# A four-layer graph network on one core: matrix for 4500 destinations instead of 5000, and four jobs moved to other queues and stages

## The chip, the cores and the metric

The kernel runs on one core of one Trainium2 chip. The metric is the time of one execution on the device, in microseconds (us). The kernel before takes 3546.83 us, the median of three runs (3539.9 to 3551.82). One more execution was taken with the hardware profiler, and all durations below come from it. PE is the matrix engine (PEld its weight loads), DVE the vector engine, ACT the scalar engine, POOL GpSimd, and SP the sync engine, which here only issues DMAs.

## The reference, cut to what matters

There are N = 6250 nodes with 128 features and E = 106250 directed edges, sorted by destination (`dst`); each node has one edge to itself at least. Four layers follow each other, each with a residual and a layernorm:

```python
edge_index = jnp.stack([src, dst])
x = _layernorm(x + _L0_gnn_ref(x, edge_attr_128, src, dst, ...))   # MLP of [sum over edges of edge_attr_128, x]
x = _layernorm(x + _L1_gnn_ref(x, edge_index, ...))                # h = (1+eps) x + sum of x[src]; MLP with two batchnorms
x = _layernorm(x + _L2_gnn_ref(x, edge_index, ...))                # two means of x[src], each with two matmuls
x = _layernorm(x + _L3_gnn_ref(x, edge_index, edge_attr_16, ...))  # attention over the edges of a node, 3 heads
```

Three sums over the edges of a node have the same form, `jax.ops.segment_sum(x[src], dst)`: one in layer 1 and two in layer 2 (called layers 2a and 2b below). Layer 3 forms a logit for each edge from three terms, `a_src[row2] + a_dst[col2] + a_edge`, with `a_edge` from `edge_attr_16` (for a node's own edge from the mean over its edges), and takes a softmax over the edges of each node.

## The kernel before, in words

**Layer 0's stage and the matrix.** 70 batches of `edge_attr_128` are loaded by SP's queue and summed by destination with one-hot matmuls (`by_group`). Into the same loop is woven `making` (L620): it builds, for the first `ND` = 5000 destinations, the 0/1 adjacency matrix from nodes to destinations, in bf16. It does so in steps: DVE makes two one-hots (`olow` and `okey`, L616), PE multiplies them (`made`, four matmuls, L643), ACT copies the product into a stage (L645) and stores that to DRAM through its own queue. There are 13 steps for 250 destinations, 260 in all. The matrix lies in DRAM as 10 parts of 500 destinations.

**An aggregation.** `neighbours` (L778) runs three times. For each of the matrix' parts it loads ten pieces of 625 KB by SP's queue, and for each piece PE makes 15 matmuls (L845; 150 for a part, features split in three bf16 pieces as the stationary operand `xp`, written by `split`). The destinations that the matrix doesn't hold (1250 of them, 61 groups) are handled by `gathered()`: `fetch` has POOL's queue gather their source rows from a table in DRAM with indirect DMAs, 128 rows each (L800; three for a group, 183 in all), eight groups' buffers deep; then for each quad of four groups PE sums with one-hots (`both`, L341), ACT copies to `by_node` (L343), PE transposes (L345) and DVE adds (L348). `due` spreads the quads over the pieces; `others()` waits for all that remain and then handles their parts. In layers 1 and 2a `others()` comes after the last part of the matrix, in layer 2b before its last two. After a part's sum, `take`/`then` do what the layer needs with its 500 destinations.

**What else shares these stages.** `logits` loads `edge_attr_16` in 28 slices (`eat`, L691 and L693) on POOL's queue during layer 1's aggregation, with the products on DVE (L683, L684). `counting` (L524) and `counted` (L549) find where each node's edges begin: an iota on POOL (L542), compares on DVE (L544, L546), small matmuls (L536), all in layer 1's aggregation; then 50 gathers of `nd` on POOL (L436) and 13 compares and reductions on DVE (L563, L564), in layer 1's MLP and layernorm. `loops` sums `a_edge` along the edges and stores `esum`; `last_sums` (L663) gathers from it 50 times (`st`, L665, POOL) in layer 2a's aggregation. In layer 2b, `then` forms for each part the rows for layer 3 and scatters `a_dst` to the first edge of each node, four indirect DMAs on POOL (`edst`, L1071); its buffers `xw` and `ad` are partly filled by POOL memsets first (L1048, L1049). Layer 3 loads `edst` (L1102), spreads it along the edges by a scan, fetches rows for all 831 tiles of edges (L1090) and works through 208 windows.

**The order.** Every engine executes its own list of instructions in a fixed order that the framework's scheduler sets when the program is built; a queue's DMAs are issued in the order of the engine that issues them. Waits are on semaphores.

Of the kernel before, what the change touches and what calls it, by code (L numbers as in the profile page):

```python
# [8 lines left out]
F32 = mybir.dt.float32  # L9
# [34 lines left out]
SC = 250  # L44
ND, Q0 = 5000, 54
AN = N - ND + SC + GW
# [163 lines left out]
def by_windows(ctx: ExitStack, tc: tile.TileContext, a: dict, out: bass.AP, consts, ix):  # L210
# [22 lines left out]
    x3 = dram.tile([NW, XW], F32, name="x3")  # L233
    edst = dram.tile([RB * L, 4], F32, name="edst")
    esum = dram.tile([RB * L, H], F32, name="esum")
# [172 lines left out]
    nc.gpsimd.memset(acc0, 0.0)  # L408
    nc.scalar.dma_start(edst.rearrange("(p t) f -> p (t f)", t=L), acc0[:RB, 0:L * 4])
    loan = [NB5 * F // 2]  # L410
# [137 lines left out]

    def counted(pool):  # L549
# [22 lines left out]
        p = (yield).tile([128, 4, F], F32, name="node_p")[:, 0, :]  # L572
        start = p[:PB, 0:NB5]
# [100 lines left out]
    def logits(pool, work):  # L674
# [11 lines left out]
        for c in range(0, L, W):  # L686
            x = work.tile([RB, W, 16], F32, name="eat")
            n = min(W, max(0, E - full - c))
            if n < W:
                nc.gpsimd.memset(x, 0.0)  # L690
            nc.gpsimd.dma_start(x[0:RB - 1], ea[0:full, :].rearrange("(p t) k -> p t k", t=L)[:, c:c + W, :])  # L691
            if n:
                nc.gpsimd.dma_start(x[RB - 1:RB, 0:n, :],  # L693
                                    ea[full + c:full + c + n, :].rearrange("(p t) k -> p t k", p=1))
# [10 lines left out]
    make = making(mkp, mps)  # L705
    product = products()
    quads, batches, LATE = ND // SC * 13, (NG + 3) // 4, 6
    for q in range(batches):
# [21 lines left out]
        if q in (8, 12):  # L730
            next(product)
    for _ in make:
        pass
    keep.close()

    with tc.tile_pool(name="l0w", bufs=2) as work, \
# [131 lines left out]
    with tc.tile_pool(name="l1", bufs=1) as wp:  # L868
# [37 lines left out]
        with tc.tile_pool(name="l1d", bufs=1) as dp, tc.tile_pool(name="l1e", bufs=4) as two, \  # L906
# [17 lines left out]
            for x in (logit, indices):  # L924
                for _ in x:
                    pass
        counts = ExitStack()
        degrees = counted(counts.enter_context(tc.tile_pool(name="l1c", bufs=1)))
        next(degrees)
        with tc.tile_pool(name="l1p", bufs=1) as lp, tc.tile_pool(name="l1w", bufs=2) as work, \  # L930
# [4 lines left out]
            for k in range(len(PARTS)):  # L935
# [11 lines left out]
                if k in (2, 4):  # L947
                    next(looped)
        batchnorm(2, s2, b2, g2, be2)
        with tc.tile_pool(name="l1x", bufs=2) as work, tc.tile_pool(name="zps", bufs=3, space=bass.MemoryType.PSUM) as zps, \  # L950
                tc.tile_pool(name="tps", bufs=2, space=bass.MemoryType.PSUM) as tp:
            last = None
            for blocks in CHUNKS:
# [7 lines left out]
                if last is not None:  # L961
                    last()
                degrees.send(work)
                layernorm(xn[:PB, b0:b0 + nb, :], z)
# [5 lines left out]
            last()  # L970
            degrees.send(zps)
        counts.close()

    with tc.tile_pool(name="l2", bufs=1) as wp, tc.tile_pool(name="l2w", bufs=2) as work, \
# [49 lines left out]

        ends = last_sums()
        neighbours(before, take, None, tables[1], len(matrix), lambda i: next(ends, None))
        for _ in ends:
            pass  # L1030


    with tc.tile_pool(name="l2bw", bufs=2) as work, \
# [8 lines left out]
        def then(k):  # L1042
            blocks = CHUNKS[k]
            b0, nb = blocks[0], len(blocks)
            x = xn[:PB, b0:b0 + nb, :]
            xw = work.tile([128, 4, XW], F32, name="xw")
            ad = work.tile([128, 4, 4], F32, name="ad")
            nc.gpsimd.memset(xw[:, :, F + H:XW], 1.0)  # L1048
            nc.gpsimd.memset(ad, 0.0)  # L1049
            s = nodes(xt[:, cols(k)], nb, tp)  # L1050
# [19 lines left out]
            for j in range(nb):  # L1070
                nc.gpsimd.indirect_dma_start(  # L1071
                    out=edst, out_offset=bass.IndirectOffsetOnAxis(ap=start_of[:PB, b0 + j:b0 + j + 1], axis=0),
                    in_=ad[:PB, j, :], in_offset=None)
# [845 lines left out]
```

## Time and profile before

| what | value |
|---|---|
| median of three runs | 3546.83 us (3539.9 to 3551.82) |
| profiled execution, its own time | 3244.44 us |
| its span in the trace | 3242.7 us |
| mean granted clock of PE | 0.892 |
| busy: PE / DVE / POOL / ACT | 2522.9 / 1720.1 / 1670.9 / 899.5 us |

The profiled execution is 302 us shorter than the median of the runs without a profiler; nothing in the trace says where these lie. By time from the span's start the stages are: layer 0's sums and the matrix, 30 to 473 us; layer 0's MLP, to 632; layer 1's aggregation, to 1021; its MLP and layernorm, to 1158; layer 2a, to 1640; layer 2b, to 2090; layer 3, to 3243. A row of the groups reads: line, engine, operation, output and inputs with shapes, count | busy time, mean duration in ns | idle time of the engine just before, with what ended it.

### The profile page before, as it was taken

How to read it: one execution, taken by the hardware profiler on the slowest of the kernel's cores; microseconds unless marked ns; L12 is line 12 of the kernel's file. 1: busy time of each engine (PE TensorE's matmuls, PEld its weight loads, DVE VectorE, ACT ScalarE, POOL GpSimd, SP SyncE). 2: the span in 40 equal slices, each digit the busy share in tenths (PEclk: the TensorE clock that was granted, in tenths of full speed). 3: DMA queues.
4: the chain of work that ended last, by engine and by line, in shares of the span. 5: the costliest groups of instructions: out<-in, count | busy, mean ns of one | idle time of the engine just before them, and what ended most of it. 6: DMA issues, size and time to landing. Idle time of an engine off the chain costs nothing.

```text
span 3242.7 us, 42918 instructions
## 1 busy us (share of the span) xinstructions
PE 2522.9 (78%) x14960; PEld 1531.4 (47%) x14960; DVE 1720.1 (53%) x4633; ACT 899.5 (28%) x1661; POOL 1670.9 (52%) x1690
## 2 busy tenths in 40 slices
PE   3888989878999576999988899566666677666665
PEld 2444446534444233454543344255555566555555
DVE  4878865469313830000031112277778688877776
ACT  0788874300001410000120001023323233333332
POOL 5000001167633467653056762467777777777773
PEclk9889889989999677999999899778888898888888
DMA  6699871377763264666366665422323333233321
GB/s 190 204 306 304 295 255 39 105 211 234 224 207 100 68 173 116 209 198 191 106 202 179 178 198 172 107 54 68 71 63 73 69 71 71 69 69 70 70 68 39
DMA packets 334829, 461.82 MB, mean 142 GB/s; under 512 B 45310, under 2 KB 219166, under 8 KB 334245
## 3 DMA queue, kind: packets, MB, share of 16 engines
q1 hardware_dynamic: 251420, 278.88, 29.7%
q0 software_dynamic: 54912, 105.86, 13.4%
q10 hardware_dynamic: 28270, 74.24, 6.2%
q8 instruction: 120, 1.97, 0.3%
q14 instruction: 107, 0.88, 0.1%
HBM read 375.30 MB, written 83.36 MB: 141 GB/s over the span
## 4 chain that ended last, share of the span: by engine, by line
PE 30%; DVE 14%; issue 7%; DMA 7%; POOL 6%; ACT 3%; DVEq 1%; ACTq 0%; POOLq 0%; SPq 0%
PE sums L845 16%; PE o L1198 6%; DMA rows<-x,srca 4%; DVE w L1186 3%; POOL rows L1090 3%; DVE w L1171 3%; POOL row L800 2%; ACT w L1188 2%; PE yp L1020 1%; PE w_p L1176 1%; DVE mx L1179 1%; PE fp L1132 1%; DMA row<-table,srca 1%; PE both L341 1%; POOL st L665 1%
## 5 line engine op out<-in xcount | busy, mean ns | idle before, releaser
L845 PE MATMUL sums<-piece,arena 125*128 125x500 bf16 x4500 | 998.2, 379 | 10.4 <-DMA piece<-edges 10.4
L1090 POOL DMA_INDIRECT rows<-x,srca x831 | 843.1, 1015 | 274.3 <-issue 173.4
L845 PEld LDWEIGHTS <-arena 125*128 125x128 bf16 x4500 | 433.4, 98 | 530.0 <-issue 49.8
L800 POOL DMA_INDIRECT row<-table,srca x549 | 537.9, 980 | 262.8 <-issue 129.4
L1198 PE MATMUL o<-rows,w 128*120 128x132 f32 x2078 | 358.1, 312 | 247.7 <-ACT w L1188 247.5
L1198 PEld LDWEIGHTS o<-rows,w 128*120 128x120 f32 x2078 | 308.1, 211 | 290.7 <-ACT w L1188 290.2
L645 ACT CAST arena<-made 128x1000 bf16<-128x1000 f32 (+1 forms) x260 | 315.6, 1277 | 58.8 <-PE made L643 57.0
L1188 ACT ACTIVATE w<-w 128x720 f32<-128x720 f32 x208 | 167.0, 803 | 435.1 <-DVE w L1186 398.2
L643 PE MATMUL made<-okey,olow 128*128 128x250 bf16 x1000 | 257.7, 400 | 35.5 <-ACT arena L645 16.5
L343 ACT COPY by_node<-both 128x128 f32<-128x128 f32 (+1 forms) x48 | 12.7, 265 | 764.0 <-PE both L341 726.9
L1176 PE MATMUL w_p<-ident,w 128*120 128x128 f32 x1248 | 200.5, 297 | 25.4 <-DVE w L1171 23.3
L1179 DVE TENSOR_REDUCE mx<-w_p 120x1 f32<-120x768 f32 x208 | 197.3, 949 | 18.3 <-PE w_p L1176 17.4
L1171 DVE TENSOR_TENSOR w<-oh,z 128x720 f32<-128x720 f32 x208 | 186.8, 898 | 8.3 <-PE o L1198 6.2
L352 DVE TENSOR_TENSOR onehot<-iota,relg 128x384 f32<-128x384 f32 x118 | 63.8, 543 | 235.8 <-PE both L341 221.7
L1186 DVE TENSOR_TENSOR w<-w,both 128x720 f32<-128x720 f32 x208 | 186.4, 896 | 3.0 <-PE both L1183 2.6
L1176 PEld LDWEIGHTS w_p<-ident,w 128*120 128x120 f32 x1248 | 159.6, 150 | 57.0 <-DVE w L1171 25.5
L716 POOL MEMSET ea<- 128x128 f32 x1 | 0.2, 208 | 357.3 <-PE sums L341 357.3
L643 PEld LDWEIGHTS <-olow 128*128 128x128 bf16 x1000 | 109.9, 119 | 157.2 <-issue 69.2
L616 DVE TENSOR_TENSOR okey<-iok,key 128x1000 bf16<-128x1000 bf16 (+1 forms) x260 | 169.4, 652 | 0.0
L1156 DVE TENSOR_TENSOR z<-rows,zed 128x12 f32<-128x12 f32 x208 | 34.1, 164 | 196.0 <-DMA rows<-x,srca 195.8
L341 PE MATMUL both<-row,onehot 128*32 128x128 f32 x1098 | 55.0, 299 | 104.1 <-DVE arena L348 60.1
L1148 PE MATMUL o<-zeros 128*120 128x380 bf16 x416 | 126.1, 351 | 10.2 <-POOL zeros L1112 8.6
(286 smaller groups left out, 3305.6 us busy)
## 6 DMA issues: line engine op xcount, KB each, us to landing
piece<-edges SPq DMA_DIRECT2D x300, 625.0 KB
edges<-arena ACTq DMA_DIRECT2D x100, 625.0 KB
ea<-in_edge_attr_dram SPq DMA_DIRECT2D x69, 768.0 KB
loop<-x SPq DMA_DIRECT2D x208, 68.0 KB
rows<-x,srca POOLq DMA_INDIRECT x831
row<-table,srca POOLq DMA_INDIRECT x549
eat<-in_edge_attr_dram POOLq DMA_DIRECT2D x28, 236.0 KB
table<-xn SPq DMA_DIRECT2D x24, 224.0 KB
```

Source lines behind the costliest of these rows:

```text
L616: nc.vector.tensor_tensor(o[:, :, 0:n], numbers[:, :, 0:n], of.rearrange("p (o g) -> p o g", o=1).to_broadcast([128, m, n]), op=OP.is_equal)
L643: nc.tensor.matmul(p[:, i, 0:NB5 * GD], lhsT=o[:, :, i], rhs=w[:, :, i], start=True, stop=True)
L645: nc.scalar.copy(to, p[:, 0:n, 0:NB5 * GD].rearrange("p i (h d) -> p i h d", d=GD))
L800: nc.gpsimd.indirect_dma_start(out=r[:, j, :], out_offset=None, in_=table, in_offset=bass.IndirectOffsetOnAxis(ap=ix["src"][:, t:t + 1], a ...
L845: nc.tensor.matmul(p, lhsT=xp[:PB, h, i, :], rhs=t[:PB, :, (h - h0) * SC:(h - h0 + 1) * SC], start=(h == 0 and i == 0), stop=(h == NB5 - 1 ...
L1090: nc.gpsimd.indirect_dma_start(out=r[:, j, :], out_offset=None, in_=x3, in_offset=bass.IndirectOffsetOnAxis(ap=ix["src"][:, BT * b + j:BT ...
L1171: nc.vector.tensor_tensor(w, oh.to_broadcast([128, S, H, BW]), z.rearrange("p j (h w) -> p j h w", w=1).to_broadcast([128, S, H, BW]), op= ...
L1176: nc.tensor.transpose(tp[:, j // 3, j % 3 * 128:(j % 3 + 1) * 128], w[:, j, :, :].rearrange("p h w -> p (h w)"), ident)
L1179: nc.vector.tensor_reduce(mx, tp[:, :, 0:384], AX.XY, OP.max)
L1186: nc.vector.tensor_tensor(wf, wf, mb.rearrange("p (j h) w -> p j (h w)", j=1) .to_broadcast([128, S, H * BW]), op=OP.subtract)
L1188: nc.scalar.activation(wf, wf, AF.Exp)
L1198: nc.tensor.matmul(o[:, 0:F + H + 1], lhsT=wf[:, j, :], rhs=rr, start=(j == 0), stop=(j == S - 1))
```

## The change

There are six edits.

1. `ND` goes from 5000 to 4500 (and `Q0` with it): nine parts of the matrix instead of ten, and 81 groups of fetched destinations instead of 61.
2. `counting` runs in layer 0's stage beside the matrix build (one of its eleven calls at batches 15, 20, ... 65), with buffers of its own; `counted` runs in layer 0's MLP.
3. The loads of `eat` are issued by ACT's queue, their memset by DVE.
4. `last_sums` issues its 50 gathers in one go at the end of layer 1's MLP.
5. `xw` and `ad` are three fixed buffers, filled once by DVE.
6. The scatters of `a_dst` alternate between two tensors; layer 3 loads both and adds them.

```diff
-ND, Q0 = 5000, 54
+ND, Q0 = 4500, 49
...
-    edst = dram.tile([RB * L, 4], F32, name="edst")
+    edst = [dram.tile([RB * L, 4], F32, name=f"edst{i}") for i in range(2)]
...
-    nc.scalar.dma_start(edst.rearrange("(p t) f -> p (t f)", t=L), acc0[:RB, 0:L * 4])
+    for x in edst:
+        nc.scalar.dma_start(x.rearrange("(p t) f -> p (t f)", t=L), acc0[:RB, 0:L * 4])
...
     def counting(pool, psum):
-        row = tail[:RB, AN:AN + M * PB]
-        view = arena[:RB, NB5 * 3 * F + 2 * (AN + M * PB):]
+        row = pool.tile([RB, M * PB], F32, name="node_row")
+        view = pool.tile([RB, 2 * M * PB], BF16, name="node_below")
...
-                p = psum.tile([128, 2 * SC], F32, name="hp1")
+                p = psum.tile([128, 256], F32, name="counts")
...
     def last_sums():
         for b in range(NB5):
             nc.gpsimd.indirect_dma_start(
                 out=st[:PB, b, :], out_offset=None, in_=esum,
                 in_offset=bass.IndirectOffsetOnAxis(ap=lasti[:PB, b:b + 1], axis=0))
-            yield
...
     def logits(pool, work):
...
-                nc.gpsimd.memset(x, 0.0)
-            nc.gpsimd.dma_start(x[0:RB - 1], ea[0:full, :]...)
+                nc.vector.memset(x, 0.0)
+            nc.scalar.dma_start(x[0:RB - 1], ea[0:full, :]...)
...
-    product = products()
+    product, indices = products(), counting(gw, pp1)
...
     for q in range(batches):
...
-    for _ in make:
-        pass
+        if q >= 13 and q % 5 == 0:
+            next(indices, None)
+    for x in (make, indices):
+        for _ in x:
+            pass
...
         nc.gpsimd.memset(xp[96:128], 0.0)
+        degrees = counted(cp)
+        next(degrees)
         for blocks in CHUNKS:            # layer 0's MLP
...
+            degrees.send(work)
         last()
+        degrees.send(yps)
...
-            logit, indices = logits(dp, two), counting(dp, hps)
+            logit = logits(dp, two)
             def each(i):                 # layer 1's aggregation
-                if i % 7 == 1:
-                    next(indices, None)
                 if i % 3 == 2:
                     next(logit, None)
...
-        degrees = counted(counts.enter_context(tc.tile_pool(name="l1c", bufs=1)))
-        next(degrees)
...
+            last_sums()                  # end of layer 1's MLP
         batchnorm(2, s2, b2, g2, be2)
...
-        ends = last_sums()
-        neighbours(before, take, None, tables[1], len(matrix), lambda i: next(ends, None))
-        for _ in ends:
-            pass
+        neighbours(before, take, None, tables[1], len(matrix))
...
+        ads = xws.tile([128, 3, 4, 4], F32, name="ad")
+        xws = xws.tile([128, 3, 4, XW], F32, name="xw")
+        nc.vector.memset(xws[:, :, :, F + H:XW], 1.0)
+        nc.vector.memset(ads, 0.0)
...
         def then(k):                     # layer 2b
-            xw = work.tile([128, 4, XW], F32, name="xw")
-            ad = work.tile([128, 4, 4], F32, name="ad")
-            nc.gpsimd.memset(xw[:, :, F + H:XW], 1.0)
-            nc.gpsimd.memset(ad, 0.0)
+            xw, ad = xws[:, k % 3], ads[:, k % 3]
...
-                    out=edst, out_offset=bass.IndirectOffsetOnAxis(ap=start_of[:PB, b0 + j:b0 + j + 1], axis=0),
+                    out=edst[j % 2], out_offset=bass.IndirectOffsetOnAxis(ap=start_of[:PB, b0 + j:b0 + j + 1], axis=0),
...
-        ed = fp.tile([RB, L, 4], F32, name="ed")
-        for p0, p1, queue in ((0, 112, nc.sync), (112, RB, nc.scalar)):
-            queue.dma_start(ed[p0:p1].rearrange("p t f -> p (t f)"),
-                            edst[p0 * L:p1 * L, :].rearrange("(p t) f -> p (t f)", t=L))
+        ed, more = (fp.tile([RB, L, 4], F32, name=n) for n in ("ed", "edm"))
+        for to, x, queue in ((ed, edst[0], nc.sync), (more, edst[1], nc.scalar)):
+            for p0, p1 in ((0, 112), (112, RB)):
+                queue.dma_start(to[p0:p1].rearrange("p t f -> p (t f)"),
+                                x[p0 * L:p1 * L, :].rearrange("(p t) f -> p (t f)", t=L))
+        nc.vector.tensor_add(ed, ed, more)
```

In the program as built, two orders follow. `st`'s gathers stand on POOL between the row fetches of layer 1 and those of layer 2a (before: in front of the second pair of quads of layer 2a). And with `nd` gone from layer 1's stage, SP issues the first five pieces of layer 2a earlier, and about 150 of layer 2a's `sums` matmuls, one part, stand in PE's list among the transposes of layer 1's layernorm (before: none).

More of the change, by code (lines that the diff above doesn't have):

```diff
@@ L571, in counted @@
             nc.vector.tensor_scalar(shift[:, i, :], iota[:PB, :PB], nxt[:PB, i:i + 1], None, op0=OP.is_equal)
-        p = (yield).tile([128, 4, F], F32, name="node_p")[:, 0, :]
+        p = (yield).tile([128, 4, F], F32, name="yp")[:, 0, :]
         start = p[:PB, 0:NB5]
@@ L689, in logits @@
             if n < W:
-                nc.gpsimd.memset(x, 0.0)
-            nc.gpsimd.dma_start(x[0:RB - 1], ea[0:full, :].rearrange("(p t) k -> p t k", t=L)[:, c:c + W, :])
+                nc.vector.memset(x, 0.0)
+            nc.scalar.dma_start(x[0:RB - 1], ea[0:full, :].rearrange("(p t) k -> p t k", t=L)[:, c:c + W, :])
             if n:
-                nc.gpsimd.dma_start(x[RB - 1:RB, 0:n, :],
+                nc.scalar.dma_start(x[RB - 1:RB, 0:n, :],
                                     ea[full + c:full + c + n, :].rearrange("(p t) k -> p t k", p=1))
@@ L731, in by_windows @@
             next(product)
-    for _ in make:
-        pass
+        if q >= 13 and q % 5 == 0:
[3 more added lines that the diff above has]
+            pass
     keep.close()
-    with tc.tile_pool(name="l0w", bufs=2) as work, \
+    with tc.tile_pool(name="l0w", bufs=2) as work, tc.tile_pool(name="l0c", bufs=1) as cp, \
             tc.tile_pool(name="hps", bufs=4, space=bass.MemoryType.PSUM) as hps, \
@@ L923, in by_windows @@
             neighbours(None, take, then, tables[0], len(matrix), each)
-            for x in (logit, indices):
-                for _ in x:
-                    pass
-        counts = ExitStack()
-        degrees = counted(counts.enter_context(tc.tile_pool(name="l1c", bufs=1)))
-        next(degrees)
+            for _ in logit:
+                pass
         with tc.tile_pool(name="l1p", bufs=1) as lp, tc.tile_pool(name="l1w", bufs=2) as work, \
@@ L962, in by_windows @@
                     last()
-                degrees.send(work)
                 layernorm(xn[:PB, b0:b0 + nb, :], z)
@@ L970, in by_windows @@
             last()
-            degrees.send(zps)
-        counts.close()
     with tc.tile_pool(name="l2", bufs=1) as wp, tc.tile_pool(name="l2w", bufs=2) as work, \
@@ L1025, in take @@
             return late
-        ends = last_sums()
-        neighbours(before, take, None, tables[1], len(matrix), lambda i: next(ends, None))
-        for _ in ends:
-            pass
-    with tc.tile_pool(name="l2bw", bufs=2) as work, \
+        neighbours(before, take, None, tables[1], len(matrix))
+    with tc.tile_pool(name="l2bw", bufs=2) as work, tc.tile_pool(name="l2bx", bufs=1) as xws, \
             tc.tile_pool(name="tps", bufs=2, space=bass.MemoryType.PSUM) as tp, \
             tc.tile_pool(name="aps", bufs=1, space=bass.MemoryType.PSUM) as aps:
+        ads = xws.tile([128, 3, 4, 4], F32, name="ad")
+        xws = xws.tile([128, 3, 4, XW], F32, name="xw")
+        nc.vector.memset(xws[:, :, :, F + H:XW], 1.0)
+        nc.vector.memset(ads, 0.0)
         for blocks in CHUNKS:
```

## The prediction, made before the changed kernel was run

> **What bounds the kernel now.** I read the busy time by stage first, then what each stage waited for, then POOL's groups in the aggregations, then the chain of waits at the end of layer 2b. Rows of the first view: stretch and its length, busy time and count of PE, PEld, DVE, ACT, POOL; granted PE clock; DMA share; GB/s. The stretches are layer 0 with the build, layer 0's MLP, layer 1's aggregation, its MLP and layernorm, 2a, 2b and layer 3.
>
> ```profile
> 30.00:480.00 450.00, 369.35 (x2830) 189.87 (x2831) 335.12 (x923) 324.99 (x335) 29.17 (x28) 0.87 0.85 273
> 480.00:632.00 152.00, 141.07 (x706) 94.00 (x704) 77.62 (x237) 65.76 (x117) 19.43 (x5) 0.97 0.18 52
> 632.00:1021.00 389.00, 355.35 (x1963) 164.44 (x1963) 181.57 (x318) 4.25 (x16) 221.74 (x248) 0.96 0.71 214
> 1021.00:1158.00 137.00, 84.14 (x238) 45.52 (x238) 106.23 (x333) 61.48 (x109) 69.28 (x55) 0.72 0.23 62
> 1158.00:1640.00 482.00, 441.55 (x2224) 217.86 (x2224) 47.95 (x130) 44.01 (x91) 233.32 (x235) 0.94 0.57 165
> 1640.00:2090.00 450.00, 379.17 (x2082) 182.95 (x2082) 94.72 (x378) 37.24 (x83) 243.69 (x262) 0.92 0.61 179
> ```
>
> PE bounds the three aggregations (0.91, 0.92 and 0.84 busy), mostly with L845. The build has no single bound. POOL is busy for half of an aggregation, but its stretch of work is longer than its busy time shows:
>
> ```profile
> L845 PE MATMUL sums<-piece,arena 125*128 125x500 bf16 x4500 | 998.2, 379 | 10.4 <-DMA piece<-edges 10.4
> L800 POOL DMA_INDIRECT row<-table,srca x549 | 537.9, 980 | 262.8 <-issue 129.4
> ```
>
> A part of the matrix is 150 matmuls of 998.2/4500 = 0.222 us; on the chain 45 take 9.5 us, so 31.7 us for a part. A row fetch is 0.98 us (1.02 in layer 1, 0.96 later) and about 0.29 of issue: 1.25 us from one to the next.
>
> What PE and POOL wait for in layer 1 (first three rows) and in layer 2b (total, times, longest):
>
> ```profile
> DVE product L683 <- DMA eat<-in_edge_attr_dram: 41.7, 5, 27.8
> PE both L341 <- DVE arena L348: 29.4, 5, 20.1
> POOL row L800 <- PE both L341: 24.1, 7, 7.0
> ...
> DVE xw L1066 <- POOL xw L1048: 138.6, 11, 25.6
> POOL edst L1071 <- DMA edst<-ad,start_of: 82.1, 33, 5.5
> PE both L341 <- DVE arena L348: 30.7, 4, 11.3
> ```
>
> In both stages PE waits some 30 us for DVE's small adds, which stand in DVE's list behind an operation that POOL is late for: in layer 1 a product whose `eat` load is queued behind row fetches, in 2b an `xw` whose memset is queued behind scatters.
>
> **The change part by part.** Everything is summed against the profiled execution (3244.4 us), then carried to the median, which is 302 us longer.
>
> *Build (edits 1, 2).* 26 of 260 steps go. In the stretch 110 to 480 a step took 370/260 = 1.42 us; PE was busy 329, ACT 305, DVE 290. DVE loses 26 x (0.65 + 0.41 + idle) = 24..28 and gains counting: 10 x (0.47 + 6 x 0.86 + 0.5) = 61; result about 325, PE 307. So DVE becomes the busiest of three engines that take turns. Bounds: all 26 steps saved (-37) and all 61 on the path with 24 saved (+37). Counting falls in the gaps of a loop in which DVE idled 45 us on `made`; I take -5. Stores to the matrix fall from 62.5 to 56.3 MB, with DMA share at 0.85 in that stretch, so they ask for nothing new.
>
> *Layer 0's MLP (2).* POOL now gathers `nd` 17 times (1.5 us each, from 63.2 us of 50 with their issue) before the 16.1 us memset of `xp`, which the first `split` needs. That memset ran at 483.1 to 499.2, and DVE then waited 8.7 us for counting's iota, which is gone. First cast at 503 before; now 466..473 + 25 + 16 = 507..515: +8 (0..+13). The 13 compares and reductions (1.4 us) replace counting's 6 us steps on a DVE that is half idle: 0, and +1 for the last little matmul.
>
> *Layer 1's aggregation (1, 2, 3).* PE: 355 - 31.7 + 5 quads x 1.1 (24 `both` 0.86, transposes 0.27) = 329. The wait on `eat` (29) goes, since ACT is busy 4 us of 389. But POOL: 243 fetches x 1.30 = 316, starting at 633, so the last row lands near 955, followed by the last quads and about 135 matmuls (28.6): end 985 instead of 1021: -35. If POOL's waits for a free buffer stay (24 us before): -15; if PE sets it alone: -45. Weighing a rule: the trace's row gives 41.7 us of DVE waits for 25 us of issue on POOL. The Trainium skill, "Trainium Kernel Development and Optimization", Key Constraints, says that DMAs of SP, ACT and POOL share 16 engines and another issuer only saves issue time. By that the edit is worth at most 25 us of POOL, and nothing where PE bounds; by the trace it is worth 29 us of PE's waits, as the loads are late from standing in line and not from bandwidth (share 0.71). I take the row.
>
> *Layer 1's MLP and layernorm (2, 4).* The layernorm was DVE-bound (82.4 of 95 us busy at 1060 to 1155); 12 compares and reductions of 1.4 us go: -16. PE takes one part of 2a's sums (31.7 us) into its list there; with its 33 us of transposes it still fits under DVE's 66, but a transpose now may stand behind 15 matmuls (3.2 us) where DVE waits for it, in 12 chunks: up to +38, some of it hidden. I take -12 for the stage (-18..+10). The 50 `st` gathers (1.5 us each, 75 us) start when `esum` has landed, some 85 us before the layernorm ends, so they are over when the first row may be fetched; if `esum` comes 20 us later, they cost 2a's first rows 10.
>
> *Layer 2a (1, 4).* Part 0 is already summed: -32. A part is gone: -31.7; five quads more: +5.5. PE waited 37 us for rows at the beginning, since 50 `st` gathers stood before them (1240 to 1280: PE 25 of 40 us); these go: -25. But fetches now pace the quads: 243 x 1.25 = 304 of some 415 us, and with part 0 gone the first four quads of 15 us come without other work beside them: +16. Sum -67 (-90..-40).
>
> *Layer 2b (1, 5, 6).* `others()` stands before the last two parts, so rows must be in by then. POOL before: 183 fetches, 21 scatters and waits, from 1645.6 to 1932.6 (287 us), last `both` at 1954, last sums 109 us later. Now 243 x 1.25 = 304, + 20 scatters of 1.5, + 4..8 of waits (they fall, as two chains alternate) = 338..345: the last row 51..58 us later in the stage. PE needs for seven parts and 21 quads only 7 x 31.7 + 23 + `then`s = 260 and waits. 18 us of slack was there (last row to last `both`), and the wait for `xw` (30 us) is gone with no use for it: +34 (0..+60).
>
> *Into layer 3 (6).* The scatters after the last sums stood in one line of about 4 us each; in two, 16.8 us on the chain fall to 9: -8. The second tensor doubles 9.12 us of loading at the most; by the Trainium skill, "DMA: Bandwidth & Descriptors", Anatomy of one DMA, a DMA takes 2 us and its bytes at 436 GB/s, so a second 1.7 MB beside the first adds 3.9 as an estimate: by the row +9, by the page +4, I take +6; the add is 3584 columns where a like DVE row took 2.96 us for 2688: +4. Sum +2. The extra clearing store at 34 us is under a stage of loads: 0..+4.
>
> Sum: -5 + 8 + 1 - 35 - 12 - 67 + 34 + 2 = -74, so 3170 in the profiled execution. In the median, -74 if its 302 us lie elsewhere, -81 in proportion, and more if PE is what is slower there (POOL then bounds less: 2b near 0, layer 1 -50: about -120). I take -87: 3460.
>
> **The rivals.**
> *POOL becomes the bound in all three aggregations.* 60 fetches more are 75 us in each. For it: 304 us of fetches against 329 of PE in layer 1 and 260 in 2b's first part, and PE's clock fell to 0.74 (664 to 700) where it waited, so waits make its work dearer. Against it: in 1 and 2a PE still has more work. It gives layer 1 -15, 2a -35, 2b +50, rest as above: -6, about 3540.
> *Slower: a hand-over for each quad.* `rows` holds two quads, so POOL may fetch a quad only when PE has done with the one two before, and PE's list is in order: once POOL bounds, each stops for the other. In layer 1 POOL waited 24.1 us for `both`, 1.6 for each of 15 quads, while PE was the bound and it cost nothing. At that price for 21 quads in three aggregations it adds 101 us to the rival above: +95, 3640. It decides from 0.3 us a quad (63 x 0.3 = 19, more than 6 + 10.6), if POOL bounds all three. Against it: in 2b POOL ran from 1645.6 to 1932.6 with 1.7 us of such waits.
> *The change does not do what it says:* the `eat` loads on ACT wait there behind `by_node` copies, which wait for `both` (311.8 us in layer 1). Then DVE's product is as late as before, the 29 us stay: 3490.
> *PE is what is slower in the runs timed:* 3425.
>
> **How the numbers follow.** Forecast 0.45 (3425..3500), `eat` still late 0.15, PE slower 0.13, POOL the bound everywhere 0.17, hand-over 0.10. Range 3385 to 3545: it leaves out the last case and a gain beyond 160; the build's bounds, -37 to +37, lie within it. Of POOL-everywhere half is faster by over 0.3% (10.6 us, about what a measurement of this kernel can tell from no change), a third the same, the rest slower. Faster 0.45 + 0.15 + 0.13 + 0.08 = 0.81, same 0.06, slower 0.13.
>
> **What would show it.** Right: no wait of `product` on `eat`; `sums` among layer 1's layernorm; layer 2a near 415 us with no wait on rows at its start but some later; in 2b PE waits for `row` before `others()`, no waits of `xw` on POOL, and waits of `edst` well under 82 us; the build ends by 475. Wrong: DVE over 0.9 busy in the build and PE waiting on `okey`; rows ending after the last sums in layer 1 (POOL bound); layernorm of layer 1 longer than before (sums in the way); layer 2b longer by over 60.

## The result and the profile after

The changed kernel takes 3645.78 us (median, 3634.74 to 3652.89), the kernel before beside it 3547.47 us: 1.028 of before, 95% interval 1.0254 to 1.0306. The prediction was 3460.

One thing has to be known to read what follows: on some occasions all runs of the kernel before took about 3240 us (the 3240 level below), on others 3520 to 3585 (the 3550 level), and every ratio here is against runs of before on the same occasion and chip. The profile of before that the prediction was made from (3242.7) was of the first, the medians that it was carried to of the second, and so is the profile after.

Before was therefore profiled again at the 3550 level. Busy time by stage there, before (first) and after, each cut at its own stage ends: build, layer 0's MLP, layer 1's aggregation, its MLP and layernorm, 2a, the gap and 2b, layer 3. The columns are stretch, length, busy time and count of PE, PEld, DVE, ACT, POOL, granted PE clock, DMA share, GB/s.

```profile
30.00:473.00 443.00, 362.39 (x2821) 185.38 (x2821) 334.64 (x923) 322.97 (x333) 29.66 (x28) 0.87 0.85 273
473.00:635.00 162.00, 145.72 (x714) 96.61 (x713) 79.82 (x240) 67.49 (x120) 22.08 (x9) 0.94 0.22 66
635.00:1023.00 388.00, 365.72 (x1963) 167.23 (x1963) 178.59 (x313) 4.23 (x16) 218.65 (x244) 0.96 0.68 212
1023.00:1172.00 149.00, 85.11 (x242) 45.73 (x240) 114.39 (x346) 61.44 (x109) 78.07 (x65) 0.69 0.28 80
1172.00:1650.00 478.00, 429.60 (x2121) 202.49 (x2122) 33.65 (x104) 33.17 (x69) 223.15 (x221) 0.91 0.51 157
1650.00:2155.00 505.00, 425.68 (x2169) 204.16 (x2166) 94.67 (x362) 46.14 (x100) 235.13 (x256) 0.91 0.52 159
2155.00:3550.00 1395.00, 861.05 (x4915) 735.87 (x4915) 880.07 (x2305) 364.75 (x911) 857.42 (x836) 0.78 0.22 56
```

```profile
30.00:480.00 450.00, 339.15 (x2771) 181.36 (x2771) 355.31 (x969) 297.60 (x307) 36.33 (x38) 0.80 0.79 258
480.00:664.00 184.00, 148.05 (x715) 96.69 (x715) 81.99 (x265) 67.82 (x120) 86.25 (x61) 0.89 0.28 82
664.00:1117.00 453.00, 355.05 (x1885) 157.40 (x1886) 150.97 (x279) 5.58 (x21) 231.88 (x236) 0.90 0.56 174
1117.00:1182.00 65.00, 56.34 (x147) 26.86 (x144) 35.30 (x96) 30.88 (x49) 15.78 (x13) 0.94 0.22 70
1182.00:1688.00 506.00, 417.37 (x2173) 201.34 (x2172) 100.59 (x326) 61.73 (x129) 288.36 (x282) 0.92 0.50 151
1688.00:2259.00 571.00, 423.56 (x2164) 199.24 (x2163) 101.57 (x390) 50.61 (x110) 291.79 (x290) 0.84 0.45 137
2259.00:3640.00 1381.00, 850.95 (x4918) 720.96 (x4916) 883.83 (x2306) 365.79 (x911) 862.22 (x836) 0.78 0.23 58
```

Layer 1's aggregation is 65 us longer although it lost 150 matmuls of `sums`, and PE stands for 98 of its 453 us (before 22 of 388). Layer 2b is 66 us longer, PE standing 147 of 571 us (79 of 505). Layer 1's MLP and layernorm and 2a, taken together because part of 2a's sums moved into the layernorm, are 56 us shorter (149 + 478 against 65 + 506). Layer 3, whose share is nearly unchanged code, differs by 14. What stands out in layer 1 of the changed kernel is the wait of DVE's products that the change was to remove (first row: before, from the view of the tile `eat`; second: after), what PE waits for (third row: before; the last two: after), and the rows of `eat` (operation, count, issue in ns as minimum/median/maximum, first and last start):

```profile
  DMA eat<-in_edge_attr_dram: 38.0, 6
DVE product L683 <- DMA eat<-in_edge_attr_dram: 68.7, 16, 7.7
...
PE both L341 <- DVE arena L348: 8.0, 2, 4.4
...
PE both L345 <- ACT by_node L343: 30.5, 5, 12.7
PE both L341 <- DVE arena L348: 30.3, 4, 9.7
```

```profile
L691 ACTq DMA_DIRECT2D eat<-in_edge_attr_dram x28: 239/240/7221, 653.5 to 881.8; - x28
L693 ACTq DMA_DIRECT2D eat<-in_edge_attr_dram x17: 391/4038/8247, 653.8 to 789.9; - x17
```

On POOL the same two issues took 0.56 and 0.54 us at the median in the profile of before at this level. On ACT the second holds the engine for 4 us at the median and up to 8, and from the eighth slice on these issues stand between the copies of `by_node` in ACT's list. ACT is busy 5.58 us in this stage, but its 45 issues of `eat`, which do not count as busy, took 107 us in all (25 on POOL before).

### The profile page after: what moved, and what is told of

It is laid out like the page before. It is cut to its first block, busy times and chain, and to the rows that moved or that the text cites. A ratio compares the mean times of both kernels' runs of the same rounds, so it can differ in the third digit from the quotient of the medians.

```text
span 3640.6 us, 42840 instructions
## 1 busy us (share of the span) xinstructions
PE 2597.5 (71%) x14785; PEld 1588.0 (44%) x14785; DVE 1729.0 (47%) x4671; ACT 884.0 (24%) x1650; POOL 1830.3 (50%) x1787
## 4 chain that ended last, share of the span: by engine, by line
PE 50%; DVE 14%; issue 12%; another core or an unknown queue 9%; DMA 7%; ACT 4%; POOL 3%; ACTq 1%; DVEq 1%; SPq 0%; POOLq 0%
PE sums L852 18%; PE o L1197 8%; DMA eat<-in_edge_attr_dram 4%; PE w_p L1175 4%; PE made L644 3%; ACT arena L646 2%; PE o L1147 2%; PE both L341 2%; PE sums L341 2%; DVE w L1185 1%; DVE mx L1178 1%; PE both L1182 1%; PE yp L1019 1%; DVE node_below L547 1%
## 5 line engine op out<-in xcount | busy, mean ns | idle before, releaser
L807 POOL DMA_INDIRECT row<-table,srca x729 | 708.0, 971 | 527.7 <-issue 175.8
L852 PEld LDWEIGHTS <-arena 125*128 125x128 bf16 x4050 | 398.3, 100 | 611.6 <-issue 215.4
L1197 PE MATMUL o<-rows,w 128*120 128x132 f32 x2078 | 399.5, 336 | 154.1 <-issue 80.9
L1197 PEld LDWEIGHTS o<-rows,w 128*120 128x120 f32 x2078 | 347.6, 234 | 196.5 <-issue 104.0
L646 ACT CAST arena<-made 128x1000 bf16<-128x1000 f32 (+1 forms) x234 | 282.5, 1272 | 67.1 <-PE made L644 58.2
L352 DVE TENSOR_TENSOR onehot<-iota,relg 128x384 f32<-128x384 f32 (+1 forms) x133 | 72.3, 545 | 409.3 <-PE sums L852 190.4
L644 PE MATMUL made<-okey,olow 128*128 128x250 bf16 x900 | 234.6, 400 | 40.1 <-ACT arena L646 18.6
L1182 PE MATMUL both<-ident,mx 120*128 120x120 f32 x208 | 73.6, 354 | 214.7 <-DVE acc L1205 130.2
L348 DVE TENSOR_TENSOR arena<-arena,both 128x32 f32 x243 | 45.3, 187 | 371.4 <-PE both L345 140.1
L341 PE MATMUL both<-row,onehot 128*32 128x128 f32 x1458 | 88.7, 306 | 138.5 <-DVE arena L348 63.3
```

The source lines that it names most:

```text
L341: nc.tensor.matmul(p[i * GW:(i + 1) * GW, :], lhsT=oh[:, i * GT + j, :], rhs=rows[i][:, j, :], start=(j == 0), stop=(j == GT - 1))
L644: nc.tensor.matmul(p[:, i, 0:NB5 * GD], lhsT=o[:, :, i], rhs=w[:, :, i], start=True, stop=True)
L646: nc.scalar.copy(to, p[:, 0:n, 0:NB5 * GD].rearrange("p i (h d) -> p i h d", d=GD))
L807: nc.gpsimd.indirect_dma_start(out=r[:, j, :], out_offset=None, in_=table, in_offset=bass.IndirectOffsetOnAxis(ap=ix["src"][:, t:t + 1], a ...
L852: nc.tensor.matmul(p, lhsT=xp[:PB, h, i, :], rhs=t[:PB, :, (h - h0) * SC:(h - h0 + 1) * SC], start=(h == 0 and i == 0), stop=(h == NB5 - 1 ...
L1197: nc.tensor.matmul(o[:, 0:F + H + 1], lhsT=wf[:, j, :], rhs=rr, start=(j == 0), stop=(j == S - 1))
```

## The experiments

Each ratio is the kernel's runs over those of before beside it, with the 95% interval. The expectations were written before each run; where one names "here" or "this chip", it is the 3240 level. The stage lengths under a verdict are read off the starts of the first and last `sums` of each aggregation, of the last `made`, and the end of the span.

**1. Which edits?** The first four ran together, with before at 3240.09 us. `b0` is before unchanged. `nd_count` has edits 1 and 2 alone, `count_only` edit 2 alone. `nd_back` undoes edit 1 in the changed kernel:

```diff
-ND, Q0 = 4500, 49
+ND, Q0 = 5000, 54
```

> The kernel before, unchanged, profiled once more, since the changed kernel's profile (3642 us) agrees with its runs and that of before (3244 us) does not agree with its own (3547 us). Theory A (the profile of before is an execution of another speed): span about 3545 us, and layer 3, whose code is nearly the same in both kernels, takes about 1330 us here instead of 1153 and 1365 in the changed kernel; granted clock about 0.84 instead of 0.892. Theory B (the profile is as the runs are, and only the runs without it are longer): span near 3245 again.

Measured: 3235.98 us, span 3234.2. On this occasion theory B holds: before runs at the speed of its profile. At the 3550 level theory A does (see 4).

> The kernel before with edits 1 and 2 alone (4500 destinations in the matrix, counting in the build, counted in layer 0's MLP; counting's old place is too small for 4500). Theory POOL-bound: nearly the whole loss, +80..+120 us (3630..3670). Theory that the loss lies in edits 3 to 6: about 3500..3550.

Measured: 0.9981 (0.9971 to 0.9991). No loss and hardly a gain: at this level the loss lies in edits 3 to 6, as the second theory had it (3500 to 3550 are 0.987 to 1.001 of 3547).

> The kernel before with edit 2 alone (counting in the build, counted in layer 0's MLP, 5000 destinations). If DVE in the build is what lost: +40..+60 us (3590..3610). If the row fetches are: -10..+10, as layer 1's layernorm gets shorter by what the build and the late memset of xp get longer.

Measured: 0.9855 (0.9838 to 0.9871), -47 us. Both expectations missed. The last `made` started at 503 us instead of 474, so counting on DVE costs 30 us where 260 steps stay, but layer 1's rest and 2a together fell from 586 to 513: with `nd` gone from layer 1, the layernorm is short and 2a's first part moves under it.

> The changed kernel with 5000 destinations in the matrix again (edit 1 undone). If 60 more fetches for each aggregation are the loss: faster than before, 3480..3530. If they are not: 3600..3650, as the changed kernel.

Measured: 1.0074 (1.0053 to 1.0095), 3262.68 us. So edits 3 to 6 take back more than edit 2 gains: 3262.68 - 3193.18 = 69.5 us. The stage shows where: layer 1's aggregation took 372 us in `count_only` and 448 in `nd_back`.

**2. Edit 3.** Four kernels beside before at 3242.98 us. `after3` is the changed kernel again. `eat_back` puts both `eat` loads on POOL (and the memset with them), `nd_eat_back` does that with 5000 destinations, and `eat_112` keeps them on ACT but splits the 118 partitions:

```diff
-            nc.scalar.dma_start(x[0:RB - 1], ea[0:full, :]...[:, c:c + W, :])
+            for p0, p1 in ((0, 112), (112, RB - 1)):
+                nc.scalar.dma_start(x[p0:p1], ea[0:full, :]...[p0:p1, c:c + W, :])
```

> The changed kernel again, beside the kernel before on the same chip. If edits add up as on this chip (edits 2 to 6 together +22 us, edit 1 on top of edit 2 +40 us): +62 us, 3300. If what made both slower in the first comparison (before 3547, after 3646) enlarges the difference: under +40. Theory of the eat loads on ACT: POOL waits over 70 us for both in layer 1, and ACT's eat issues take several us each.

Measured: 1.0068 (1.0044 to 1.0092), 3266.29 us: slower, but by 23 us and not 98. In layer 1 POOL waits 77.1 us for `both`, as the theory of `eat` had it.

> The changed kernel with edit 3 alone undone (the eat loads on POOL's queue again). Theory eat on ACT (its in-order list holds by_node behind loads that issue slowly): layer 1's aggregation falls from some 455 us to some 380, total -70 against the changed kernel, about 3230. Theory that the row fetches make layer 1 long: -0..-15, since POOL gets 25 us of issue back.

Measured: 0.9943 (0.9915 to 0.9972), 3227.61 us: 39 us less than `after3` and layer 1's aggregation 382 us against 421. The place was right, the size a little over half of what was expected.

> The changed kernel with each eat load on ACT split into 112 and 6 partitions (before: one DMA of 118). Theory of the spread over engines (a hardware queue's DMA of 118 = 2 x 59 partitions goes to two of the 16 DMA engines, one of 112 = 16 x 7 to all): the issue of the last partition's load, 4.7 us now, falls to under 1 us and most of the 70 us come back, about 3240. Theory of ACT's order alone (loads stand behind by_node and by_node behind loads): no gain, 3300, or worse for 28 more DMAs.

Measured: 0.9851 (0.983 to 0.9873), 3194.17 us: 72 us less than `after3`, with 28 DMAs more. Layer 1's aggregation took 349 us. The issues, and DVE's idle time before the products, in the view of the tile `eat`, first of `after3` and then of this kernel:

```profile
L693 ACTq DMA_DIRECT2D eat<-in_edge_attr_dram x17: 392/5129/8250, 648.9 to 785.5; - x17
...
  DMA eat<-in_edge_attr_dram: 95.3, 24
```

```profile
L692 ACTq DMA_DIRECT2D eat<-in_edge_attr_dram x56: 271/326/537, 647.2 to 794.4; - x56
L694 ACTq DMA_DIRECT2D eat<-in_edge_attr_dram x17: 229/262/268, 648.0 to 729.7; - x17
...
  DMA eat<-in_edge_attr_dram: 1.1, 1
```

5.13 us have become 0.26, and 95.3 us of waits 1.1; PE's wait for `by_node`, 31.7 us in `after3`, is gone, and POOL's for `both` is 2.1. The loads and the copies of `by_node` stand in the same order on ACT in both, so the order alone is not the cause; the shape of the DMA is. The Trainium skill has a rule that fits, in "DMA: Bandwidth & Descriptors", section Why a DMA increments its semaphore by 16 and not by 1: a hardware queue's DMA uses the largest number of engines up to 16 that divides its slowest dimension, which is 2 for 118 = 2 x 59 and 16 for 112, while some that POOL issues use 16 whatever the count. The packets of ACT's queue agree (queue, packets, MB and share in the whole execution; `after3`, then `eat_112`):

```profile
q10 hardware_dynamic: 30478, 77.95, 6.5%
...
q10 hardware_dynamic: 31038, 77.95, 6.8%
```

The same bytes took 560 packets more, all of 4 bytes: 560 = 28 x (16 + 6 - 2), one for each engine that the rule adds. And while this queue moved `eat`, `after3` had one or two packets under way in 96% of the time, `eat_112` up to 20; it was at work for 188 us in the one and 59 in the other. With the mean of the 2 KB packets on ACT's queue in `after` and `nd_back`, 0.094 us, 59 packets one after another are 5.5 us, an estimate near the 4.0 to 5.1 us (medians in three profiles) for which the next issue was held.

> The changed kernel with edits 1 and 3 undone (5000 destinations, eat on POOL); edits 2, 4, 5, 6 remain. Edit 2 alone gave 3193. Expected 3175..3195: fewer waits in layer 2b (it took 401 us with edits 5 and 6 and 419 without), 13 us more on the way into layer 3.

Measured: 0.9857 (0.9834 to 0.9879), as `count_only` without edits 4, 5 and 6. These three together are worth nothing in the sum: the gap and 2b fell from 452 to 431 us, and layer 3 from the last sums on rose from 1174 to 1185.

**3. Layer 2b and layer 0's MLP.** Four kernels, all with `eat` split, beside before at 3531.74 us: the 3550 level. `best_5000` has 5000 destinations. The core of the others:

```diff
-        neighbours(None, take, then, tables[2], len(matrix) - 2)
+        neighbours(None, take, then, tables[2], len(matrix) - 1)
```

```diff
-        nc.gpsimd.memset(xp[96:128], 0.0)
+        nc.vector.memset(xp[96:128], 0.0)
```

```diff
-                    for j in range(GT):
+                    for j in range(1 if table is tables[2] else GT):
```

They are `late_others`, `mem_dve` and `one_fetch`, in that order.

> The changed kernel with the eat loads split at 112 and 5000 destinations again. If the 60 more fetches are worth their while once eat comes in time: slower than the 3194 with 4500, about 3210. If layer 2b loses more by them (it took 494 us with 4500 and 431 with 5000) than layers 1 and 2a win (348 against 374; about 506 against 514): 3165..3180.

Measured: 0.984 (0.9814 to 0.9866), between the two expectations (as ratios 0.990, and 0.976 to 0.981). With `eat` in time 5000 destinations are better at this level, by the next two runs.

> The changed kernel with the eat loads split at 112 and, in layer 2b, the fetched destinations due before the last part of the matrix instead of before the last two. Theory that POOL's fetches bound 2b up to that point: PE gets 31.7 us of other work in the meantime and 2b shortens by 20..30, 3170. Theory that what comes after (four gathered parts in a row, then the last part) sets the end: 0 or slower, 3190..3210.

Measured: 1.0151 (1.0114 to 1.0187). No gain; the gap and 2b took 559 us, and 556 in `eat_112_2` below without the edit.

> The changed kernel with the eat loads split at 112 and the memset of xp on DVE instead of POOL. Theory that the memset behind 17 gathers of nd on POOL, and DVE standing for its 16 us, holds layer 0's MLP: -15..-25, about 3175. If PE's MLP bounds there anyway: 0.

Measured: 1.0149 (1.0122 to 1.0177). Layer 0's MLP fell from 184 us (`after`, `eat_112_2`) to 165, but the sum does not show it: `eat_112_2`, on another occasion, has 1.0145.

> The changed kernel with the eat loads split at 112, fetching in layer 2b only the first of each group's three tiles and using it three times (the sums over fetched destinations of that aggregation are not those of the reference). 162 of 243 fetches go there. If POOL bounds 2b up to others(): rows end by some 260 us of the stage instead of 340 and the stage shortens by 60..90, about 3120. If PE or the chain after it bounds: 0..-15.

Measured: 0.9693 (0.9663 to 0.9724). Layer 2b from 2a's last sums to its own took 382 us, against 556 to 570 in the three kernels at this level that differ from it by the fetches and one other line at most. 162 fetches fewer are worth some 173 us or more, over 1 us each and twice the 60 to 90 us expected: to that extent they are what 2b waits for. (The kernel leaves out two of the three fetches of each group in 2b and computes other sums there.) In this stage PE is busy nearly throughout:

```profile
1650.00:2040.00 390.00, 377.37 (x2203) 190.28 (x2201) 102.07 (x392) 50.27 (x111) 138.29 (x128) 0.98 0.59 174
```

**4. Edit 1 at the 3550 level.** The next four ran there too, with before at 3564.09 us. `b0_2` is before again, the source of the first windows above; `nd_back_2` and `eat_112_2` repeat `nd_back` and `eat_112`; `best_mem` is `best_5000` with the memset on DVE.

> The kernel before, unchanged, for one more profile. The changed kernel took 3642 us in one profile and 3265 in another; in the longer one PE starts instructions 0.70 us apart for stretches of some 20 us in layers 1 and 2, and in layer 3 stands for 2.5 to 4.7 us at a time. If before runs at 3240 here: none of these, as in its first profiles. If it runs at some 3540: the same two patterns, some 50..80 us of the first and some 180 of layer 3, which would make them a property of the execution and not of the change.

Measured: 3551.84 us, span 3550.0, with both patterns: 83 us of starts 0.70 or 1.40 us apart (counted as below), and layer 3 at 1396 us instead of 1178. They belong to the occasion or the chip and not to the change.

> The changed kernel with 5000 destinations again (edit 1 undone). Where before takes 3240 it took 1.007 of it, as long as the changed kernel. Where before takes some 3540, theory that edit 1 carries the loss there (180 fetches more in stages where PE is slow with its rows): about before, 0.995..1.01, against 1.028. Theory that eat on ACT carries it: 1.02..1.03.

Measured: 1.0059 (1.0038 to 1.008), against 1.028 of the changed kernel on its own occasion. Edit 1 carries some four fifths of the loss at this level, (1.028 - 1.0059) / 0.028.

> The changed kernel with the eat loads split at 112 again. Where before takes 3240 it took 0.985. Where before takes some 3540, theory edit 1: still 1.015 (as two kernels that differ from it in one line took there). Theory eat: under 0.99.

Measured: 1.0145 (1.01 to 1.0191). With `eat` in time, edit 1 costs 3% at this level: 1.0145 against 0.984 of `best_5000`, and 1.015 (`late_others`, `mem_dve`) against the same 0.984 on one occasion.

> 5000 destinations, eat loads split at 112 on ACT, the memset of xp on DVE, the other edits kept. Each of these alone went the right way: the 5000 and split took 0.984 where before takes 3531; the memset moved the start of layer 1's sums from 182 to 165 us after the build. Expected: 0.975..0.980 of before on either kind of execution (3165 or 3455).

Measured: 0.9778 (0.9717 to 0.9839), 3489.78 us: the lowest ratio of the kernels that compute everything. Its interval overlaps that of `best_5000`, so a gain by the memset is not shown. It was not run at the 3240 level.

**5. A hand-over?** In `eat_112_2` POOL waits for `both` 33 us and for `sums` 43 us in layer 1, and PE for rows: each could be standing for the other. `deep_4500` (from `eat_112`) and `deep_5000` (from `best_mem`) got a third quad of buffers, with before at 3563.28 us:

```diff
-tc.tile_pool(name="rows", bufs=8) as rp
+tc.tile_pool(name="rows", bufs=12) as rp
...
                 fetch(quads[0])
+                fetch(quads[1])
                 for q in quads:
-                    if q != quads[-1]:
-                        fetch(q + 1)
+                    if q + 2 <= quads[-1]:
+                        fetch(q + 2)
```

> The changed kernel with the eat loads split at 112, and buffers for three quads of fetched rows instead of two, fetched two quads ahead. It took 1.0145 of before where before takes some 3540, and 0.985 where it takes 3240. Theory of the hand-over (PE stands for rows, POOL then stands for PE's buffers: 76 us for PE in layer 1, 27 to 54 in 2b): 0.995..1.005 of before on the slower kind of execution. Theory that PE's slow stretches alone set it, or POOL's pace alone: 1.01..1.02 there; on the faster kind 0.98..0.985 by either.

Measured: 1.0218 (1.0178 to 1.0258).

> The kernel with 5000 destinations, eat split, memset on DVE, and three quads of rows. Without the third quad it took 0.978 of before on the slower kind of execution, where POOL waited 80 us for PE in layer 1 and 55 in 2b. Theory of the hand-over: 0.97; theory that PE's matmuls bound with 5000 destinations: 0.978 again.

Measured: 0.9897 (0.9852 to 0.9943). Neither gains by the third quad: `deep_5000` is slower than `best_mem`, and the interval of `deep_4500` overlaps that of `eat_112_2`. POOL's waits for `both` in layer 1 fell from 33.2 to 18.2 us, and the aggregation went from 423 to 426. The hand-over theory, which expected 0.995 to 1.005 and 0.97, falls.

## Why the prediction was wrong, point by point

The stages, from profiles of before and after at the same level (`b0` and `after3`; `b0_2` and the changed kernel's first profile):

| step | predicted | at 3240 | at 3550 |
|---|---|---|---|
| build | -5 | +2 | +7 |
| layer 0's MLP | +9 | +22 | +22 |
| layer 1's aggregation | -35 | +36 | +66 |
| layer 1's rest and 2a | -79 | -79 | -57 |
| 2b with the gap before it | +34 | +47 | +68 |
| from the last sums to the end | +2 | +4 | -14 |
| sum | -74 | +31 | +91 |

(The stages are read off single starts and rounded, so they differ from the cuts above by up to 2 us, and the sums, which are those of the spans, by 1 from the column.)

Two steps failed: the term for `eat` in layer 1 (a wait of 29 us that goes), and the price of the 500 destinations that edit 1 moves to the fetches, which was to fall in the median, "POOL then bounds less", and which was 3% of the time at the level of the runs.

*Layer 1's aggregation: the step that failed first.* The prediction said "The wait on `eat` (29) goes, since ACT is busy 4 us of 389", and weighed the right kind of page against the trace: the rule that another issuer saves only issue time would have given 0 there. I took the trace's row, which shows loads late from standing in POOL's line, but did not ask how the same DMA goes on another kind of queue, and a low busy time does not say that issues will be quick, since they are not in it. ACT's issue was held, `by_node` and PE behind it, and loads came no sooner: -35 became +36 at 3240. There the size itself was sound: in `eat_112`, where the loads are in time, the stage took 349 us against 384 of before, -35. At 3550 it was not: `eat_112_2` took 423 us against 388 of before and 453 of the changed kernel, so the shape of the loads is some 30 of the 101 us by which the forecast missed. Edit 1 is 51: `best_mem`, with 5000 destinations on the same occasion, took 372. And the 29 us were not there to be gained: PE's wait for DVE's adds is 8.0 us in `b0_2` (the row above) where the prediction's profile has 29.4. The rival "the change does not do what it says" named this wait and kept the 29 us; its reason, the order on ACT, is not the one that `eat_112` shows, and it missed that ACT holds `by_node`, hence PE, while it issues.

*Layer 2b: the second.* The price of 60 fetches on POOL was right at 3240: rows took 339 us from first to last (predicted 338 to 345, before 283). Its effect on the end was +47, not +34. The first row stood 45 us behind 2a's last sums and not 37 (+8), which the prediction had at nothing; the rows took 57 us more; of the slack of 18 us 10 were used, as the last `both` came 6 us after the last row and not 16; and from there to the last sums it took 8 us less. At 3550 the rows took 406 us, against 322 of before there, and the end moved by +68.

*Layer 0's MLP.* The memset began 27 us after the last `made` (501.7 against 475.0), where it was 10 before (483.4 against 473.5). The wait behind it did go, as predicted: the first cast came at 517.9, directly behind it, where it was 503.5 before, 4 us behind. That is +14 for the +8 of the prediction, which had the build end by 473. From there to layer 1's first sums another 9 us went, where it had 1; why is not shown.

```profile
L740 POOL MEMSET arena<- x1: 16092/16092/16092, 483.4 to 483.4; 32x19200 bf16 x1
...
L743 POOL MEMSET arena<- x1: 16092/16092/16092, 501.7 to 501.7; 32x19200 bf16 x1
```

(The first row is of `b0`, the second of `after3`, in the view of the memset's line.)

*What held.* Counting took the 26 steps' place in the build (+2 for -5). Layer 1's rest and 2a came out within 1 us at the 3240 level, and not by luck: the layernorm ended 12 us sooner behind layer 1's last sums (predicted 12), and 67 (predicted 67) came in 2a. POOL's waits for the scatters fell from 77.9 to 22.3 us (`b0`, `after3`), though 2b did not end sooner by it. Into layer 3, at 3240, +4 for +2 has two parts: the first load of `edst` came 10 us sooner behind the last sums (predicted 8), but from it to the scan it took 15 us more (predicted 10). The loads are 9 of these (20.4 us from the first issue until the add can start, against 11.7 until the scan), as the row had it; the page's +4 was too small, and its figure is given for DMAs that POOL issues, while these are issued by SP and ACT.

*From the profile to the median.* The prediction allowed for PE being slower in the 302 us and concluded "POOL then bounds less", for a larger gain (-87 and not -74). PE is slower there, but the sign of what follows was wrong: instead of layer 1 at -50 and 2b near 0, +66 and +68. Compare one quad in 2b, in the changed kernel with `eat` split: first at the 3240 level, then at the 3550 level (`mem_dve`). The columns are start, length, instruction, and in brackets the idle time before it.

```profile
1710.46 0.42 PE L341 MATMUL both<-row,onehot 128*32 128x128 f32 x6
1711.90 0.65 PE L341 MATMUL both<-row,onehot 128*32 128x128 f32 x16 [1.02 <-DMA row<-table,srca]
1714.85 0.63 PE L341 MATMUL both<-row,onehot 128*32 128x128 f32 x2 [2.31 <-DMA row<-table,srca]
```

```profile
1888.14 0.37 PE L341 MATMUL both<-row,onehot 128*32 128x128 f32 x1 [0.98 <-issue]
1889.54 0.37 PE L341 MATMUL both<-row,onehot 128*32 128x128 f32 x1 [1.03 <-issue]
1890.94 0.37 PE L341 MATMUL both<-row,onehot 128*32 128x128 f32 x1 [1.03 <-issue]
1893.04 0.37 PE L341 MATMUL both<-row,onehot 128*32 128x128 f32 x1 [1.73 <-issue]
```

In the first, PE waits for two rows and then runs 16 matmuls in 0.65 us. In the second it goes on one by one, 1.4 and 2.1 us from start to start, though nothing is shown that it waits for. The whole quad took from 1879.7 to 1901.4, at a granted clock of 0.59 (1.00 in the 22 us before). Such stretches, counted in layers 1 and 2 as successive starts on PE and PEld within 0.01 us of 0.70 or 1.40 us apart, are 0 to 2 us in every profile at the 3240 level and 47 to 150 us in those at the 3550 level. They are longer with more fetches in `eat_112_2` (123 us) than in `best_mem` (56), though the changed kernel has 90 and before 83; longer still with the third quad (150 in `deep_4500`), and there are none in 2b of `one_fetch`. At this level a destination moved from the matrix to the fetches costs more than the matmuls that it saves. The stages of one occasion show it: from `best_mem` to `eat_112_2` layer 1's aggregation grows by 51 us, 2a with what is before it by 32, 2b by 69, and the build shrinks by 28. That the slow stretches are the reason is argued from where they lie, and not shown.

*The rivals.* "POOL becomes the bound" holds for 2b, as `one_fetch` shows; for 1 and 2a no run tests it, but PE was busy 331 of 350 us in layer 1 of `eat_112`. "A hand-over for each quad" gave 3640, nearly the result, but by luck: its mechanism is one that the third quad refutes.

*What stays open.* What makes the two levels was not tried. Each of the five chips on record shows one level only (two of them 3240, three 3550), so the chip may be it as well as the occasion; and the mean granted clock of before is 0.829 to 0.853 in its runs at 3550 and 0.873 to 0.894 in those at 3240, which may be cause or consequence. Nor is it settled whether PE's slow stretches come from the waits for rows or from the fetches beside them: `one_fetch` takes away both. The changed kernel at 1.028 and `nd_back_2` at 1.0059 ran on different occasions of the same level, so the share of four fifths rests on ratios and not on one comparison.

## What to carry to other kernels

Before a DMA is moved from POOL to a hardware queue, look at its outer count: 118 partitions cost this kernel 72 us at the 3240 level that 112 and 6 did not. An engine that issues DMAs is held by a slow issue, which its busy time does not show, and so is all that stands behind it in its list: ask who waits for those. And a profile whose time is not that of the runs may show other waits than they have: profile both kernels at the level of the runs before work is traded between engines. Handing 500 destinations to the fetches cost nothing at one level (1.0068 of `after3` against 1.0074 of `nd_back`) and 2.2% at the other (1.028 against 1.0059); with `eat` on POOL it cost 0.9% at the first (`eat_back` against `nd_eat_back`), with its loads split 3% at the second.

## What the hardware showed that I had not expected

- PE at the 3550 level starting instructions 0.70 us apart, or a multiple, for some 20 us at a time; in `mem_dve` one such stretch runs from 1879.7 to 1901.4, with all its waits but one labelled "issue", while POOL goes on fetching at its usual 1.25 us.
- Layer 3 at that level takes 1378 to 1414 us instead of 1174 to 1185, with PE busy 861 us instead of 751 for the same instructions and a granted clock of 0.78 instead of 0.84 (`b0_2`, the last row of the first windows above, and `b0`, here), while DVE's and POOL's busy times differ by 1 to 2%.

```profile
2056.00:3234.00 1178.00, 750.57 (x4920) 636.82 (x4917) 862.88 (x2305) 359.08 (x911) 847.21 (x836) 0.84 0.26 67
```

- A memset on POOL and a normalization on DVE in `count_only`: four instructions that take 1.16 us in `after`, where they end before the memset, took 17.05 us, and end with the 16.1 us of the memset.

```profile
528.98 17.05 DVE L300 TENSOR_SCALAR xn<-y,mv,rstd 125x128 f32<-125x128 f32 x4
...
L743 POOL MEMSET arena<- x1: 16100/16100/16100, 529.8 to 529.8; 32x19200 bf16 x1
```
